# A two-direction selective scan on one core: the gate product issued after the scan of its slot, and the dt projection with its softplus moved by one slot

## The chip, the cores and the metric

The kernel runs on one core of one Trainium2 chip. The core has a matrix engine (PE, with a separate record for its weight loads, PEld), a vector engine (DVE), an activation engine (ACT), a general engine (POOL) and a queue that issues transfers (SP), each with its own instruction stream; sixteen DMA engines carry the transfers. The metric is the device time in microseconds (us). The time before is 8892.45 us, the median of three runs (8888.39 to 8895.94).

## The reference

The input is (1, 64, 256, 128): 64 channels, 256 times, 128 frequencies, in 32-bit floats. Layer 0 runs a pair of selective state-space blocks (one forward, one on the reversed sequence) along time, and then another pair along frequency. One block is, cut to what matters:

```python
xz = einsum('nld,ed->nle', rmsnorm(u), in_proj_w); x, z = split(xz, 2)
x  = silu(causal_conv4(x) + conv_b)
dt, B, C = split(x @ x_proj_w.T, [4, 4 + 16])
dt = softplus(dt @ dt_proj_w.T + dt_proj_b)
h_t = exp(dt_t * A) * h_{t-1} + dt_t * B_t * x_t      # 128 channels x 16 states
y_t = sum over states of h_t * C_t
out = ((y + x * Dp) * silu(z)) @ out_proj_w.T + u
```

The two directions are concatenated, projected to 64 channels and added to the input. Layer 1 is a normalisation, a convolutional LSTM over 32 windows and a projection. It isn't touched here.

## The kernel before

Layer 0 is done by the class `Stage`, once for time (stage 0, sequences of 256) and once for frequency (stage 1, sequences of 128). A stage has 64 **chunks** of 512 tokens. A chunk has 16 **slots**: two directions d of eight slots each, and each slot takes eight channels of all 16 states twice, as one tile of 128 partitions by 1024. The slot is named by its number in the chunk, 0 to 15.

The order of the work is written out by hand: `run` (L524) walks over all slots of a stage, and every engine takes its instructions in the order in which this loop writes them. In slot S it writes:

- `gate` (L480), when S is 2 or 10: y times silu(z), on DVE, for the direction that ended two slots before;
- `times_b` for S+1 on DVE (L437): the driving term, in PSUM, times B;
- `recur` on DVE (L443): the scan of 1024 steps, 2.28 us, that makes h;
- `outputs` for S-1 on POOL (L456): h times C;
- `inputs` for S+2 on PE (L416): it spreads dt*x over the states into one of three PSUM tiles `bx`, and `decays` for S+2 on ACT (L430): exp(A*dt), two activations into one of four tiles;
- `add_up` for S-2 on PE (L471), in odd slots: the sum over states of two h tiles into y. There is one y tile in PSUM, and its first matmul in a direction is L464;
- `close_a` in slot 2 (L491) and `close_b` and `keep` in slot 3 (L500, L510 or L517): the output projection of the chunk before, and its copy into X;
- at last the steps that prepare the next chunk, which `head` (L369) puts into slots.

The steps of `head` and the slot of the running chunk in which each stands:

| step | engine, line | slots before (d=0; d=1) |
|---|---|---|
| `squares`, `means`, `rms` | ACT L256, PE L261, ACT L266 | 12, 13 |
| `normalise` | POOL L272, then a copy of `unp` by DMA (L273), issued on SP | 14 |
| `project_x` | PE L281 and L282, reads `unp`; ACT L283 | 0; 4 |
| `project_z` | PE L288, ACT L296 | 1; 5 |
| `silus` | ACT, two table loads (L301, L306), four activations (L305) | 5 |
| `project_dt`, `softplus_a` | PE L310; ACT L321 to L323 (abs, relu, exp) | 6; 9 |
| `softplus_b` | ACT L329 to L331 (1+e, its log, and back) | 7; 10 |
| `softplus_c` | POOL L334, L335 | 8; 11 |
| `softplus_d` | POOL L339, then four writes of dt to DRAM (L343), issued on SP | 9; 12 |
| `times_x` | POOL L348 | 9; 12 |
| `project_bc` and `keep_bc`, first B, then C | PE L354, ACT L358 | 7, 8; 10, 11 |
| `spread_dt`, four of 1 MB in each direction | DMA L364 into three tiles `rep`, issued on SP | 10, 12, 14, 0; 2, 4, 6, 8 |

All projections of `head` and the output projection share one PSUM tile (tag `mm`), so each of them waits until the one before has been read. Where two steps stand in one slot, those of the earlier chunk come first, and within a chunk the order of the `put` calls holds. So in slot 14 the spread of dt stands on SP ahead of the copy of `unp`.

## Time and profile before

| what | value |
|---|---|
| median of three runs | 8892.45 us |
| profiled execution | 8909.66 us, its span 8907.9 us |
| busy PE, DVE, POOL, ACT | 7263.5, 7220.8, 6371.9, 5230.0 us |
| mean granted PE clock | 0.946 |
| span from 220 to 3950 us (most of stage 0): busy DVE, POOL, PE, ACT | 3385.4, 3024.2, 2976.9, 2475.3 of 3730 us |
| span from 8000 us (layer 1): busy PE | 894.2 of 908 us |

In the profile a row of a group gives the line, the engine, the operation and its tiles, the number of instructions, their busy time and mean duration in nanoseconds, and after the second bar the time the engine stood idle just before them with what ended most of it. In the timeline a row gives start, length, engine and line. SPq is the queue that issues transfers: its length is the time of issuing, and the data move later. The page's busy shares of the engines are means over the whole span. They don't say which of them sets the period of a chunk.

### The profile page before, as it was taken

The numbers are of one execution on the slowest core, as the hardware profiler recorded it, in microseconds if no ns is written. First come the engines' busy times: TensorE is split into PE (matmuls) and PEld (weight loads), VectorE is DVE, ScalarE is ACT, GpSimd is POOL, SyncE is SP. The second block draws the span as 40 slices with busy tenths as digits, with TensorE's granted clock in tenths as the row PEclk, the third lists the DMA queues.
The fourth block names the chain that finished last, engine by engine and source line by source line (L and its number), as shares of the span: only waits on it lengthen the run. The fifth ranks groups of instructions, "written<-read, shape, count | busy, mean of one in ns | idle before, by whom it ended". The sixth has DMA issues, their size and how long they took to land. (4 is left out here: it accounts for less than half of the span.)

```text
span 8907.9 us, 80273 instructions
## 1 busy us (share of the span) xinstructions
PE 7263.5 (82%) x24548; PEld 2187.8 (25%) x24548; DVE 7220.8 (81%) x4671; ACT 5230.0 (59%) x9321; POOL 6371.9 (72%) x3351
## 2 busy tenths in 40 slices
PE   7888787887888887868787878878787888599999
PEld 2222222222222222212222222222222222145554
DVE  6999999999999999969999999999999999711112
ACT  5666666666666666646666666666666666511111
POOL 5888888888888888868888888888888888511111
PEclk8999999999999999979999999999999999899999
DMA  5766676666666666656666666666666666400000
GB/s 126 160 153 151 157 161 156 154 155 158 157 156 150 159 159 153 154 115 154 152 149 152 156 151 151 154 155 150 149 157 151 151 153 154 106 13 9 9 9 10
DMA packets 238749, 1186.43 MB, mean 133 GB/s; under 512 B 39376, under 2 KB 64624, under 8 KB 107248
## 3 DMA queue, kind: packets, MB, share of 16 engines
q1 hardware_dynamic: 238320, 1181.30, 57.8%
q8 instruction: 197, 3.23, 0.2%
q14 instruction: 232, 1.90, 0.1%
HBM read 1088.88 MB, written 75.50 MB: 131 GB/s over the span
## 5 line engine op out<-in xcount | busy, mean ns | idle before, releaser
L456 POOL TENSOR_TENSOR h<-h,bc 128x1024 f32<-128x1024 f32 x2048 | 4807.9, 2360 | 942.9 <-DVE h L443 932.9
L443 DVE TENSOR_TENSOR_SCAN h<-dA,bx 128x1024 f32<-128x1024 f32 x2048 | 4659.7, 2275 | 0.0
L416 PE MATMUL bx<-dtx,sel 64*128 64x512 f32 x8192 | 2636.3, 680 | 504.6 <-DVE h L443 500.8
L430 ACT ACTIVATE dA<-rep,A 128x510 f32<-128x510 f32 (+1 forms) x4096 | 2699.8, 711 | 27.9 <-DVE h L443 24.6
L437 DVE TENSOR_TENSOR bx<-bx,bc 128x1024 f32<-128x1024 f32 x2048 | 2480.2, 1211 | 288.6 <-PE bx L416 235.9
L471 PE MATMUL y<-h,fold 128*32 128x512 f32 x8192 | 1364.2, 649 | 145.8 <-POOL h L456 145.8
L416 PEld LDWEIGHTS bx<-dtx,sel 64*128 64x128 f32 x8192 | 741.5, 195 | 2061.3 <-issue 1157.2
L354 PE MATMUL pb<-xs,wbc 128*128 128x512 f32 x1024 | 627.9, 697 | 440.1 <-ACT dt L322 253.8
L718 PE MATMUL pg<-xn,acc 128*128 128x456 f32 x2048 | 815.8, 549 | 0.7 <-ACT gxe L645 0.7
L755 POOL TENSOR_TENSOR a<-a,c 128x488 f32<-128x488 f32 x31 | 53.4, 1722 | 935.7 <-DVE n L777 794.9
L283 ACT ACTIVATE xs<-px,cb 128x512 f32<-128x512 f32 x256 | 176.0, 687 | 919.0 <-PE px L282 919.0
L777 DVE TENSOR_SCALAR n<-v,slope 128x512 f32<-128x512 f32 x64 | 31.1, 487 | 775.9 <-ACT v L775 774.8
L334 POOL TENSOR_TENSOR e<-e,w 128x512 f32<-128x512 f32 x256 | 326.9, 1277 | 454.2 <-ACT w L331 428.3
L482 DVE TENSOR_TENSOR yz<-y,zs 128x512 f32<-128x512 f32 x256 | 176.7, 690 | 446.4 <-PE y L471 446.1
L281 PE MATMUL px<-unp,g 128*128 128x512 f32 x512 | 305.0, 679 | 231.3 <-DMA unp<-unp 223.7
L310 PE MATMUL pv<-xs,wdt 128*128 128x512 f32 x512 | 303.5, 676 | 227.6 <-ACT xs L305 226.3
L471 PEld LDWEIGHTS y<-h,fold 128*32 128x32 f32 x8192 | 192.4, 111 | 1185.9 <-POOL h L456 585.3
L775 ACT ACTIVATE v<-pproj,bpr 128x512 f32<-128x512 f32 x32 | 22.0, 687 | 774.2 <-PE pproj L770 774.2
L718 PEld LDWEIGHTS pg<-xn,acc 128*128 128x128 f32 x2048 | 375.4, 188 | 372.3 <-issue 349.0
L354 PEld LDWEIGHTS pb<-xs,wbc 128*128 128x128 f32 x1024 | 159.8, 196 | 943.0 <-ACT dt L322 510.8
L358 ACT COPY bc<-pb 128x512 f32<-128x512 f32 x512 | 295.3, 577 | 112.9 <-PE pb L354 104.1
L348 POOL TENSOR_TENSOR dtx<-dt,xs 128x512 f32<-128x512 f32 x256 | 325.2, 1270 | 20.1
(129 smaller groups left out, 6164.1 us busy)
## 6 DMA issues: line engine op xcount, KB each, us to landing
rep<-there SPq DMA_DIRECT2D x1024, 1024.0 KB
there<-dt SPq DMA_DIRECT2D x1024, 64.0 KB
unp<-unp SPq DMA_DIRECT2D x128, 128.0 KB
u<-in_x SPq DMA_DIRECT2D x64, 128.0 KB
out<-y SPq DMA_DIRECT2D x32, 256.0 KB
w<-in_W_ih_f SPq DMA_DIRECT2D x5, 512.0 KB
w<-in_W_ih_b SPq DMA_DIRECT2D x5, 512.0 KB
cw<-in_conv_w SPq DMA_DIRECT2D x4, 128.0 KB
```

The lines of the kernel that those rows point to most:

```text
L281: nc.tensor.matmul(self.seqs(px), lhsT=m.G1[i], rhs=self.unp[:, :, first : first + L], start=True, stop=False)
L310: self.nc.tensor.matmul(self.pv, lhsT=self.m.Wdt[2 * self.stage + d], rhs=self.at["xs", ch, d], start=True, stop=True)
L334: self.nc.gpsimd.tensor_sub(self.e, self.e, self.w)
L348: self.nc.gpsimd.tensor_mul(dtx, self.dt, self.at["xs", ch, d])
L354: self.nc.tensor.matmul(self.pbc, lhsT=wt, rhs=self.at["xs", ch, d], start=True, stop=True)
L416: self.nc.tensor.matmul(bx[:, j], lhsT=self.m.sel[rows, r, k], rhs=dtx[rows], start=True, stop=True)
L430: nc.scalar.activation(dA[:, j, :, live], self.seqs(rep[:, r + 2 * j])[:, :, live], AF.Exp, scale=m.A[:, i, g : g + 1])
L437: self.nc.vector.tensor_mul(bx, bx, self.at["B", ch, d].unsqueeze(1).to_broadcast([P, 2, NTOK]))
L443: self.nc.vector.tensor_tensor_scan(h.rearrange("p j n -> p (j n)")[:, step], self.dA[S % NRING].rearrange("p j n l -> p (j n l)")[:, step ...
L456: self.nc.gpsimd.tensor_mul(h, h, self.at["C", ch, d].unsqueeze(1).to_broadcast([P, 2, NTOK]))
L471: nc.tensor.matmul(y[32 * r : 32 * r + 32], lhsT=m.fold[:, k], rhs=hs[r % 2][:, r // 2], start=False, stop=k == NK - 1, skip_group_check=True,
L718: nc.tensor.matmul(pg[:, :, 2 : 2 + inner], lhsT=acc[:, q, gate * P : (gate + 1) * P], rhs=xv[:, rows, half, q : q + inner], start=q == 0, ...
```

## The change

The `gate` of slots 2 and 10 is written after `recur` of the same slot instead of ahead of `times_b` and `recur`. In `head` the projection of dt with `softplus_a` moves from slots 6 and 9 to 7 and 10. For d=0 `softplus_b` stays in slot 7, straight after `softplus_a`, and `softplus_c` (8), `softplus_d` and `times_x` (9) stay; for d=1 all of these move one slot on, to 11, 12 and 13. The projections and copies of B and C move one slot on in both directions, to 8 and 9 and to 11 and 12. The spreads of dt stay in their slots.

```diff
         for d in range(2):
-            s = 6 + 3 * d
+            s = 7 + 3 * d
             put(s, self.project_dt, d)
             put(s, self.softplus_a, d)
-            put(s + 1, self.softplus_b, d)
+            put(s + d, self.softplus_b, d)
             put(s + 1, self.project_bc, d, 0)
             put(s + 1, self.keep_bc, d, 0)
-            put(s + 2, self.softplus_c, d)
+            put(s + 1 + d, self.softplus_c, d)
             put(s + 2, self.project_bc, d, 1)
             put(s + 2, self.keep_bc, d, 1)
-            put(s + 3, self.softplus_d, d)
-            put(s + 3, self.times_x, d)
+            put(s + 2 + d, self.softplus_d, d)
+            put(s + 2 + d, self.times_x, d)
             for k in range(4):
                 put(12 + 8 * d + 2 * k - 2, self.spread_dt, d, k)
...
-            if S % 8 == 2 and S > 8:
-                self.gate(*self.where(S - 8)[:2])
             if 0 <= S + 1 < last:
                 self.times_b(S + 1)
             if 0 <= S < last:
                 self.recur(S)
+            if S % 8 == 2 and S > 8:
+                self.gate(*self.where(S - 8)[:2])
```

## The prediction

> **What bounds the kernel now.** I read the groups of instructions first. They show DVE without a wait before its scan (L443) and with two waits before other work: 446.4 us before the gate product (L482), 288.6 us before the product with B (L437).

> ```profile
> L443 DVE TENSOR_TENSOR_SCAN h<-dA,bx 128x1024 f32<-128x1024 f32 x2048 | 4659.7, 2275 | 0.0
> L437 DVE TENSOR_TENSOR bx<-bx,bc 128x1024 f32<-128x1024 f32 x2048 | 2480.2, 1211 | 288.6 <-PE bx L416 235.9
> L334 POOL TENSOR_TENSOR e<-e,w 128x512 f32<-128x512 f32 x256 | 326.9, 1277 | 454.2 <-ACT w L331 428.3
> L482 DVE TENSOR_TENSOR yz<-y,zs 128x512 f32<-128x512 f32 x256 | 176.7, 690 | 446.4 <-PE y L471 446.1
> ```

> A chunk of 16 slots needs of DVE 16 x 3.31 us (scan to scan) plus 2 x 0.61 for the gates: 54.2 us. The gates of slot 2 follow each other in the timeline at 58.46 us in most chunks of stage 0 (58.70 in stage 1; the means with the disturbed chunks are 59.03 and 59.63). So each chunk has 4.3 us in which DVE isn't the bound, and the question is what closes that period. Here is the timeline of one chunk, cut to the steps that release one another (start, length, engine, line).

> ```profile
> 1996.94 1.28 POOL L334 TENSOR_TENSOR e<-e,w 128x512 f32<-128x512 f32 x1 [3.16 <-ACT w L331]
> 2013.96 1.28 POOL L339 TENSOR_TENSOR dt<-lw,dt 128x512 f32<-128x512 f32 x1
> 2015.27 1.72 SPq L343 DMA_DIRECT2D there<-dt  x4
> 2016.56 4.67 POOL L456 TENSOR_TENSOR h<-h,bc 128x1024 f32<-128x1024 f32 x2
> 2017.03 0.52 SPq L364 DMA_DIRECT2D rep<-there  x1
> 2021.20 1.27 POOL L272 TENSOR_TENSOR unp<-u,rs 64x512 f32<-64x512 f32 x1
> 2022.50 0.64 SPq L273 DMA_DIRECT2D unp<-unp  x1
> 2025.05 1.10 PE L281 MATMUL px<-unp,g 128*128 128x512 f32 x2 [1.65 <-DMA unp<-unp]
> 2029.16 0.69 DVE L482 TENSOR_TENSOR yz<-y,zs 128x512 f32<-128x512 f32 x1 [1.33 <-PE y L471]
> 2033.23 1.13 PE L416 MATMUL bx<-dtx,sel 64*128 64x512 f32 x4 [0.25 <-DVE h L443]
> 2042.44 1.12 PE L288 MATMUL pz<-unp,wz 64*128 64x512 f32 x2
> 2043.60 0.59 ACT L296 COPY zs<-pz 128x512 f32<-128x512 f32 x1 [1.14 <-PE pz L288]
> 2055.38 1.27 POOL L334 TENSOR_TENSOR e<-e,w 128x512 f32<-128x512 f32 x1 [3.15 <-ACT w L331]
> ```

> The reader is to see a closed loop in which each engine is back to back: POOL from its wait for softplus (1996.94) to the end of the normalise (2022.47), 25.5 us; the shift copy of unp to the first matmul on it, 2.6 us; PE from there (2025.05) to the end of the last z product (2043.56), 18.5 us with one gap of 0.26 us at 2033.23; ACT through silus, decays and both halves of softplus to POOL's next start, 11.8 us. Together 58.4, the period. The gate's wait at slot 2 (1.33) and the waits in slots 9 and 10 (0.82 and 1.84) are where DVE's slack shows. They are not what sets the period.

> Last, busy time in short stretches around the shift copy, issued at 2022.50. The three last fields are PE's granted clock, the DMA share and GB/s:

> ```profile
> 2018.00:2022.00 4.00, 2.82 (x12) 0.62 (x12) 4.00 (x3) 3.51 (x8) 4.00 (x3) 1.00 0.96 230
> 2022.50:2023.00 0.50, 0.50 (x4) 0.07 (x2) 0.50 (x1) 0.00 (x0) 0.50 (x1) 1.00 0.51 98
> 2023.00:2023.50 0.50, 0.40 (x2) 0.00 (x0) 0.50 (x1) 0.00 (x0) 0.50 (x1) 1.00 0.02 0
> 2024.00:2025.00 1.00, 0.00 (x0) 0.00 (x0) 1.00 (x2) 0.00 (x0) 1.00 (x2) 1.00 0.92 286
> 4095.00:4099.00 4.00, 4.00 (x8) 0.89 (x6) 1.96 (x1) 1.76 (x4) 4.00 (x3) 0.57 0.78 172
> ```

> The 1 MB spread (rep) issued at 2017.03 drains at about 2022.9; only then does the small copy move. It fits with no room to spare. The last line is another chunk, where PE had waited 1.93 us for unp: afterwards the granted clock is 0.57, and that chunk took 60.37.

> [...] laying its matmuls on a 3.41 us grid, all 74 windows busy under 0.40 are followed by a half-clock window, 117 of 165 between 0.40 and 0.50, and 32 of 1837 above 0.60.

> **The change part by part**, per chunk, with P the moment px can start (2025.05).

> *Gate behind the scan.* No instruction is added or removed. Product 3 now can start when inputs(3) ends (2028.07), not after add_up and gate (2029.77), 1.7 us sooner. But the next PE work isn't waiting for that: PE goes on with z product, inputs and close_a to about P+7.9, so inputs(5) starts at 2032.95 instead of 2033.23. Gain on the loop 0.3 us. The gate's own 0.61 comes after scan 2 (about P+6.4 to 7.1); what waits for it, the new y (P+8.9) and close_b (P+11), is later. With that cover gone it would cost up to 0.61. At slot 10 both the gate and its wait lie in slack: 0.

> *Softplus a and b together, one slot later (d=0).* ACT's work between silus and POOL's start is the same: two decays, six activations. Before, a decay stood between exp and the w that needs it (pitch 0.52); now they touch, and the dependent pitch of lw to w is 0.66 to 0.71: +0.17 us on the loop. The dt matmul, in slot 7 at about P+22.6 to 23.7, is ahead of ACT's need at about P+26.4 (z product's end 18.2, copy, table loads and silus 5.4, two decays 2.8): 0. The B and C products and copies one slot later are due at slots 15 and 17: 0. They leave PE and DVE small waits in slots 9 to 12, inside DVE's slack of over 4 us.

> *d=1 one slot later.* POOL's own sum stays 25.5, as the same products run in another order: outputs(12) now comes before softplus_d, not after times_x. So dt is ready one product (2.34) later, at 2017.6. With it on SP's queue, in order: four writes of dt (1.72) to 2019.3, then the 1 MB rep of slot 14, issued at 2019.4 instead of 2017.03, then unp, still issued at 2022.5. Rep takes 1.05 MB / 230 GB/s = 4.6 us from 1.2 us after its issue: 2020.6 to 2025.2. Unp's 0.13 MB, 1.1 us, ends at 2026.3 and px starts 0.45 later, at 2026.75: **+1.7 us** on the loop. Bounds: 0 if the small copy passes the large one, 4.6 if it waits for all of it.

> *What is late next: PE's clock.* PE's idle time before px grows from 1.65 to about 3.4 us. A grid of 3.41 us windows then has one with 0.55 or more idle in about 9 phases of 10. Stage 1 already shows the slope: with 1.93 us instead of 1.65, 26 of 62 chunks took over 60 us, against 9 of 61 in stage 0. One slow window on this back-to-back chain cost 60.37 - 58.70 = 1.65 us; some fall partly into the wait, so 0.92 x 1.4 = 1.3 a chunk. Of the present excess of the means (0.57 and 0.93, 0.75 together) I take all to be of this kind and subtract it: **+0.55**. Bounds: 0 and 1.65 + 1.65 (two windows).

> Sum: 1.7 - 0.3 + 0.17 + 0.55 = 2.1 us for each of 2 x 63 chunks that prepare a next one: 126 x 2.12 = 267 us. The profiled execution of 8909.66 (span 8907.9) becomes 9177. It stands 17 us above the median of 8892.45, which becomes 9160. The second layer, 900 us at the end, is untouched.

> **The rivals.**
> (B) The copy is late but the slow windows are no more than now: 126 x 1.57 = 198, 9090. For it: the grid's phase is free, and a longer loop could keep px off bad phases. Against: the idle time equals a whole window.
> (C) The copy isn't held up: 126 x (0.17 - 0.3) = -16, 8876, no change that counts. It needs unp to overtake rep, or rep to end by 2023.5; rep would have to move in 3 us what took 4.6.
> (D) The other side: the gate's wait is real loss and DVE is the bound. Then 446 us leave: 8446. It decides if product 3, ready 1.7 us sooner, moved PE's chain as much; at 2033.23 the profile shows only 0.26 us of it.
> (E) Both upper ends together, unp 4.6 late and two slow windows each time: 126 x (4.6 - 0.3 + 0.17 + 3.3 - 0.75) = 885, 9777. For it speaks only that both depend on the same wait.

> **Chances.** Forecast 0.58, B 0.25, C 0.08, D 0.05, E 0.04. Within the forecast the delay (1.3 to 2.1) and the slow windows (0 to 1.4 net) give 9080 to 9270; B reaches down to about 9030. The range 8990 to 9300 holds nearly all of these two, some 0.8. A difference of 0.2% (18 us) is about what this kernel's measurement can tell from none. Faster: D and a tail of C, 0.08; within 0.2%: the rest of C, 0.05; slower 0.87.

> **What would show it.** In the changed profile: the wait before L482 nearly gone, that before L437 grown beyond 446 + 289 us in place of it; L281's wait for unp, 223.7 us now, near 430; rep of slot 14 issued about 3 us before unp instead of 5.5; more half-clock windows just after px, mean clock under 0.946; scan and product durations unchanged. The prediction is wrong if px starts within 2.7 us of the normalise, if slot-2 gates stand closer than 58.4 us, or if PE has gaps between px and the last z product.

## The result and the profile after

The changed kernel takes 9306.45 us (median of four runs, 9298.78 to 9308.66) against 8894.19 us of the kernel before (8888.39 to 8897.46). The ratio is 1.0463, interval 1.0445 to 1.0481: it is 4.6% slower. The sign and the place were forecast, the size wasn't: 412 us were lost where 267 were predicted.

The profiled execution took 9298.78 us, with a span of 9297.0 and a mean granted PE clock of 0.918 (before: 8909.66, 8907.9 and 0.946). The span grew by 389 us, which is 3.1 us for each of the 126 chunks that prepare a next one. These are the groups of instructions after, as far as they changed or answer those shown of before, with the row of the first product on `unp` (L281):

```profile
L443 DVE TENSOR_TENSOR_SCAN h<-dA,bx 128x1024 f32<-128x1024 f32 x2048 | 4662.1, 2276 | 41.7 <-issue 41.7
L437 DVE TENSOR_TENSOR bx<-bx,bc 128x1024 f32<-128x1024 f32 x2048 | 2488.5, 1215 | 1047.1 <-PE bx L416 992.4
L281 PE MATMUL px<-unp,g 128*128 128x512 f32 x512 | 383.5, 840 | 477.0 <-DMA unp<-unp 377.2
L482 DVE TENSOR_TENSOR yz<-y,zs 128x512 f32<-128x512 f32 x256 | 170.4, 666 | 9.3 <-PE y L471 9.3
```

The work itself costs what it did: the scan takes 2.276 us, the product with B 1.215. DVE's wait of 446.4 us before the gate (L482) is 9.3 now. In its place the wait before the product with B grew from 288.6 to 1047.1, which is 312 us over the two waits of before together (735.0). A wait that moves like this says that DVE isn't the bound. Where the time goes shows in the row of L281. This is that row in the kernel before:

```profile
L281 PE MATMUL px<-unp,g 128*128 128x512 f32 x512 | 305.0, 679 | 231.3 <-DMA unp<-unp 223.7
```

PE's idle time before it was 231.3 us and is 477.0, and one such matmul now takes 840 ns instead of 679. PE comes later to this product, and then runs it at half clock more often: in both traces one such matmul takes 0.67 us in the median at a granted clock of 1.00 and 1.06 at 0.50, and 188 of the 512 ran wholly at 0.50 after, 30 before.

The timeline of one chunk after, cut to the steps of the loop (start, length, engine, line, and in brackets the idle time before it with its releaser):

```profile
2051.78 1.27 POOL L334 TENSOR_TENSOR e<-e,w 128x512 f32<-128x512 f32 x1 [4.19 <-ACT w L331]
...
2071.13 1.27 POOL L339 TENSOR_TENSOR dt<-lw,dt 128x512 f32<-128x512 f32 x1
2074.18 0.52 SPq L364 DMA_DIRECT2D rep<-there  x1
2076.02 1.26 POOL L272 TENSOR_TENSOR unp<-u,rs 64x512 f32<-64x512 f32 x1
2077.31 0.64 SPq L273 DMA_DIRECT2D unp<-unp  x1
2081.96 1.18 PE L281 MATMUL px<-unp,g 128*128 128x512 f32 x2 [2.15 <-POOL h L456]
2082.93 1.91 PE L282 MATMUL px<-unp,g 128*128 128x512 f32 x2
...
2086.67 1.23 DVE L437 TENSOR_TENSOR bx<-bx,bc 128x1024 f32<-128x1024 f32 x1 [3.39 <-PE bx L416]
2090.00 0.67 DVE L482 TENSOR_TENSOR yz<-y,zs 128x512 f32<-128x512 f32 x1
...
2101.83 0.59 ACT L296 COPY zs<-pz 128x512 f32<-128x512 f32 x1 [1.14 <-PE bx L416]
...
2113.74 1.27 POOL L334 TENSOR_TENSOR e<-e,w 128x512 f32<-128x512 f32 x1 [4.01 <-ACT w L331]
```

This is the loop of the prediction, and it can be read link by link. POOL, from its wait for softplus (2051.78) to the end of the normalise (2077.28), takes 25.5 us as before. The copy of `unp`, from there to the first matmul on it (2081.96), takes 4.7 us instead of 2.6. PE, from there to ACT's copy of the last z product (2101.83), takes 19.9 instead of 18.5. ACT, up to POOL's next start (2113.74), takes 11.9 instead of 11.8. On SP's queue the 1 MB spread was issued 3.1 us ahead of the copy of `unp`; before it was 5.5.

The busy time in short stretches around the copy shows the other half. A row gives the stretch and its length, the busy time of PE, PEld, DVE, ACT and POOL with the number of instructions, and at last PE's granted clock, the DMA share and GB/s:

```profile
2075.50:2079.50 4.00, 3.38 (x10) 0.70 (x10) 2.74 (x2) 0.00 (x0) 4.00 (x3) 0.51 1.06 254
2079.50:2081.90 2.40, 0.31 (x2) 0.00 (x0) 2.04 (x2) 0.00 (x0) 2.40 (x3) 1.00 1.02 205
2083.30:2084.30 1.00, 1.00 (x2) 0.00 (x0) 0.00 (x0) 0.00 (x0) 1.00 (x2) 0.50 0.94 213
```

In the first stretch the DMA engines are full with the spread (a share of 1.06; PE's granted clock is 0.51 there too). In the second, PE is busy for 0.31 of 2.40 us: it waits for `unp`. In the third, after this idle time, PE works at a granted clock of 0.50, in the middle of the chain that everything waits for.

I measured the four links in every chunk of the profiled executions. The table gives their means in us over the 63 chunks of a stage that prepare a next one (stage 0; stage 1), with those of four experiments that follow. The PE link ends at the start of ACT's copy of the last z product, so the four add up to the period by construction.

| kernel | POOL | copy of unp | PE chain | ACT to POOL's start | period |
|---|---|---|---|---|---|
| before | 25.40; 25.66 | 2.96; 2.86 | 18.83; 19.26 | 11.8 | 58.98; 59.56 |
| after | 25.39; 25.66 | 4.98; 4.69 | 20.22; 19.98 | 11.9 | 62.51; 62.25 |
| gate moved alone | 25.41; 25.67 | 2.87; 2.87 | 18.51; 18.51 | 11.8 | 58.57; 58.83 |
| after, spread behind unp | 25.39; 25.65 | 2.61; 2.62 | 18.66; 18.48 | 11.9 | 58.59; 58.68 |
| after, PE kept busy | 25.40; 25.67 | 5.26; 4.90 | 18.23; 18.11 | 11.9 | 60.81; 60.60 |
| normalise one slot sooner | 23.13; 23.39 | 4.73; 4.86 | 18.26; 18.23 | 11.8 | 57.90; 58.27 |

In the PE chain after, PE stands idle for only 0.04 us of 20.2 and 20.0 in the mean, and its granted clock there is 0.898 and 0.902 (before: 0.3 and 0.4 us idle, 0.985 and 0.961). So the longer chain is slower matmuls and not waits inside it.

### The profile page after: what moved, and what is told of

The parts are those of the page before. It is cut to its first block, busy times and chain, and to the rows that moved or that the text cites. A ratio compares the mean times of both kernels' runs of the same rounds, so it can differ in the third digit from the quotient of the medians.

```text
span 9297.0 us, 80527 instructions
## 1 busy us (share of the span) xinstructions
PE 7533.1 (81%) x24548; PEld 2253.7 (24%) x24548; DVE 7244.1 (78%) x4671; ACT 5267.7 (57%) x9321; POOL 6366.1 (68%) x3351
## 5 line engine op out<-in xcount | busy, mean ns | idle before, releaser
L456 POOL TENSOR_TENSOR h<-h,bc 128x1024 f32<-128x1024 f32 x2048 | 4799.6, 2357 | 1232.8 <-DVE h L443 1127.1
L443 DVE TENSOR_TENSOR_SCAN h<-dA,bx 128x1024 f32<-128x1024 f32 x2048 | 4662.1, 2276 | 41.7 <-issue 41.7
L437 DVE TENSOR_TENSOR bx<-bx,bc 128x1024 f32<-128x1024 f32 x2048 | 2488.5, 1215 | 1047.1 <-PE bx L416 992.4
L416 PE MATMUL bx<-dtx,sel 64*128 64x512 f32 x8192 | 2719.3, 684 | 445.5 <-DVE h L443 429.5
L430 ACT ACTIVATE dA<-rep,A 128x510 f32<-128x510 f32 (+1 forms) x4096 | 2698.6, 711 | 56.0 <-DMA rep<-there 35.1
L471 PE MATMUL y<-h,fold 128*32 128x512 f32 x8192 | 1512.0, 664 | 353.8 <-POOL h L456 352.7
L416 PEld LDWEIGHTS bx<-dtx,sel 64*128 64x128 f32 x8192 | 763.3, 195 | 2037.5 <-issue 1339.3
L281 PE MATMUL px<-unp,g 128*128 128x512 f32 x512 | 383.5, 840 | 477.0 <-DMA unp<-unp 377.2
L334 POOL TENSOR_TENSOR e<-e,w 128x512 f32<-128x512 f32 x256 | 327.9, 1281 | 557.9 <-ACT w L331 532.0
L471 PEld LDWEIGHTS y<-h,fold 128*32 128x32 f32 x8192 | 203.3, 112 | 1537.5 <-POOL h L456 782.7
L282 PE MATMUL px<-unp,g 128*128 128x512 f32 x512 | 366.4, 808 | 0.0
L296 ACT COPY zs<-pz 128x512 f32<-128x512 f32 x256 | 150.0, 586 | 347.6 <-PE bx L416 272.5
L335 POOL TENSOR_TENSOR lw<-lw,e 128x512 f32<-128x512 f32 x256 | 326.2, 1274 | 20.1
```

Of the source, the lines that this page charges most:

```text
L281: nc.tensor.matmul(self.seqs(px), lhsT=m.G1[i], rhs=self.unp[:, :, first : first + L], start=True, stop=False)
L282: nc.tensor.matmul(self.seqs(px), lhsT=m.G2[i], rhs=self.unp[:, :, second : second + L], start=False, stop=True)
L334: self.nc.gpsimd.tensor_sub(self.e, self.e, self.w)
L335: self.nc.gpsimd.tensor_add(self.lw, self.lw, self.e)
L416: self.nc.tensor.matmul(bx[:, j], lhsT=self.m.sel[rows, r, k], rhs=dtx[rows], start=True, stop=True)
L430: nc.scalar.activation(dA[:, j, :, live], self.seqs(rep[:, r + 2 * j])[:, :, live], AF.Exp, scale=m.A[:, i, g : g + 1])
```

## Experiments

### Which part of the change costs the time

Each experiment is set beside runs of the kernel before that were made next to it; their medians lie between 8886.84 and 8897.24 us.

Four kernels take the change apart. First the gate alone, on the kernel before:

```diff
-            if S % 8 == 2 and S > 8:
-                self.gate(*self.where(S - 8)[:2])
             if 0 <= S + 1 < last:
                 self.times_b(S + 1)
             if 0 <= S < last:
                 self.recur(S)
+            if S % 8 == 2 and S > 8:
+                self.gate(*self.where(S - 8)[:2])
```

> The kernel before with the gate alone moved behind the scan of its slot. Loop theory (the loss comes from the copy of unp queued behind the 1 MB spread, and from the halved PE clock after the longer wait): this part only takes 0.3 us off the loop, 126 x 0.3 = 38 us, so about 8856, and the copy still lands some 2.6 us after the normalise. Rival G (the gate behind the scan costs time): up to the whole 412 us, at least the 0.61 us of each of 256 gates, 9050 to 9306. Rival H (the steps of d=0 drawn together or moved make ACT and PE late in slots 7 to 10): no change, 8894.

It took 8838.28 us, 0.9937 of before (0.9922 to 0.9952). So this part is a gain of 56 us, where 38 were expected. The row of the product with B, in the groups of this kernel:

```profile
L437 DVE TENSOR_TENSOR bx<-bx,bc 128x1024 f32<-128x1024 f32 x2048 | 2488.1, 1215 | 606.8 <-PE bx L416 555.4
```

The wait before the gate is 8.9 us here, and the one in this row takes 318 us more than before: of the 437 us that the gate no longer waits, DVE waits 318 at the product with B. Another 30 went to new idle time before the scan and 12 to longer busy time. What is left, 77 us, is about the 74.5 by which this profiled execution's span (8833.4) is shorter.

Then the moves of `head` alone, with the gate left in its old place:

```diff
-            s = 6 + 3 * d
+            s = 7 + 3 * d
...
-            put(s + 1, self.softplus_b, d)
+            put(s + d, self.softplus_b, d)
...
-            put(s + 2, self.softplus_c, d)
+            put(s + 1 + d, self.softplus_c, d)
...
-            put(s + 3, self.softplus_d, d)
-            put(s + 3, self.times_x, d)
+            put(s + 2 + d, self.softplus_d, d)
+            put(s + 2 + d, self.times_x, d)
```

> The kernel before with the moved head steps alone, the gate where it was. Loop theory: the changed kernel without the 0.3 us a chunk that the gate gives, 9306 + 38 = about 9344; the copy lands 4.6 to 5 us after the normalise. Rival G: about 8894. Rival H: about 9306.

It took 9378.36 us, 1.0545 (1.0529 to 1.0561), 484 us more than before and 34 more than expected: the gate, worth 56 us alone, is worth some 72 beside these moves.

The smallest edit that holds the supposed cause moves only the end of softplus and dt\*x of d=1 from slot 12 to 13, in the kernel before:

```diff
-            put(s + 3, self.softplus_d, d)
-            put(s + 3, self.times_x, d)
+            put(s + 3 + d, self.softplus_d, d)
+            put(s + 3 + d, self.times_x, d)
```

> The kernel before with nothing changed but softplus_d and times_x of d=1 one slot later (12 to 13). Loop theory: this alone puts the writes of dt and the spread of slot 14 one POOL product later, so the whole loss is here: 2.0 us of copy and about 1.3 us of slow clock a chunk, about 9310. Rivals G and H: about 8894, since neither the gate nor the steps of d=0 are moved.

It took 9358.22 us, 1.0520 (1.0502 to 1.0537): 464 of the 484 us are in these two steps of one direction (48 us more than expected). Its timeline at the copy, cut to the two transfers and what stands around them:

```profile
2024.59 0.52 SPq L364 DMA_DIRECT2D rep<-there  x1
2026.42 1.27 POOL L272 TENSOR_TENSOR unp<-u,rs 64x512 f32<-64x512 f32 x1
2027.72 0.64 SPq L273 DMA_DIRECT2D unp<-unp  x1
2032.49 1.84 PE L281 MATMUL px<-unp,g 128*128 128x512 f32 x2 [3.85 <-DMA unp<-unp]
```

The spread is issued 3.13 us ahead of the copy, the first matmul on `unp` starts 4.80 us after the normalise ended, and the two of its line take 1.84 us instead of 1.10 (in the chunk of the changed kernel the two of L282 took 1.91 at a granted clock of 0.50).

The counter-test puts these two steps of d=1, and `softplus_c` with them, back into their old slots in the changed kernel, and leaves everything else as changed:

```diff
-            put(s + 1 + d, self.softplus_c, d)
+            put(s + 1, self.softplus_c, d)
...
-            put(s + 2 + d, self.softplus_d, d)
-            put(s + 2 + d, self.times_x, d)
+            put(s + 2, self.softplus_d, d)
+            put(s + 2, self.times_x, d)
```

> The changed kernel with softplus_c, softplus_d and times_x of d=1 back in slots 11 and 12; all else as changed (the gate, the dt projections, the two halves of softplus of d=0 together, the products with B and C). Loop theory: POOL's order and SP's order are those of before, so only the gate's gain and ACT's 0.14 us a chunk remain: the gate alone (8838) + 126 x 0.14 = about 8856. Rival H (the steps of d=0 and the later products of B and C take a share of the loss): 8900 or more.

It took 8850.68 us, 0.9956 (0.9939 to 0.9972). The dt projection one slot later, the softplus halves together and the later B and C products together cost 13 us over the gate alone (8838.28 beside 8894.24, and 8850.68 beside 8894.00), which the two intervals hardly tell from nothing.

### Is it the spread that stands ahead of the copy?

In the changed kernel, only the one spread that was put ahead of the copy of `unp` is issued a slot later, and so behind it. POOL's order stays, and nothing else moves.

```diff
-                put(12 + 8 * d + 2 * k - 2, self.spread_dt, d, k)
+                put(12 + 8 * d + 2 * k - 2 + (d == 0 and k == 2), self.spread_dt, d, k)
```

> The changed kernel with one of the eight spreads of dt (d=0, the third) issued in slot 15 instead of 14, so that on SP it stands behind the copy of unp instead of ahead of it. Loop theory: the copy lands about 2.3 to 2.6 us after the normalise again, PE's wait and the half-clock windows fall back to what they were, and only ACT's 0.14 us and the gate's gain of 0.3 remain: about 8875, at most 8930. Rivals G and H: nothing of what they blame is touched, so 9280 to 9310.

It took 8819.53 us, 0.9918 (0.9903 to 0.9932). The whole loss is gone: the kernel is 75 us faster than before, and 55 faster than was expected. The timeline at its copy, cut in the same way:

```profile
2012.74 1.27 POOL L272 TENSOR_TENSOR unp<-u,rs 64x512 f32<-64x512 f32 x1
2014.04 0.64 SPq L273 DMA_DIRECT2D unp<-unp  x1
2014.72 6.44 SPq L364 DMA_DIRECT2D rep<-there  x3
2016.63 1.10 PE L281 MATMUL px<-unp,g 128*128 128x512 f32 x2 [1.68 <-DMA unp<-unp]
```

The copy is first in the queue now, and PE starts 2.62 us after the normalise ended. The later spread still comes in time for the decays that read it: ACT's wait for the spreads before its decays (L430) is 32.0 us in all, and 35.1 in the changed kernel. This separates the order on SP from every other account: POOL's work, the later dt and the later B and C are all still there, and cost nothing that shows. It also takes away a loss that was there before: the copy now comes to PE 2.61 and 2.62 us after the normalise in the mean, against 2.96 and 2.86 before, and more than 2.8 us after it in 2 of 126 chunks against 35.

The spread behind the copy could have shared the DMA engines with it. To see whether it does, the spread of slot 0 was issued in slot 1 in the changed kernel:

```diff
-                put(12 + 8 * d + 2 * k - 2, self.spread_dt, d, k)
+                put(12 + 8 * d + 2 * k - 2 + (d == 0 and k == 3), self.spread_dt, d, k)
```

> The changed kernel with the spread that follows the copy of unp on SP (d=0, the fourth) issued one slot later, in slot 1 instead of 0. It asks why the copy came 2.0 us later and not the 1.7 of the prediction. If the copy shares the engines with the spread behind it: it lands some 0.3 us sooner, 126 x 0.3 = 38 us less than the changed kernel, about 9268. If only the spread ahead of it counts: no change, 9306.

It took 9308.05 us, 1.0465 (1.0446 to 1.0483), the time of the changed kernel, and its copy comes no sooner (5.07 and 4.79 us after the normalise). Of the spreads next to the copy, only the one ahead of it counts.

### How much of the loss is PE's clock?

Three extra matmuls stand ahead of the first product on `unp` of each chunk in the changed kernel. They write into the same PSUM tile, and the real product then overwrites what they wrote. The order on SP's queue stays, but they fill most of PE's idle time before it. The lines below them are numbered 4 higher.

```diff
+        for _ in range(3 if d == 0 else 0):
+            nc.tensor.matmul(
+                px, lhsT=m.Wdt[i], rhs=m.sel[:, 0].rearrange("p k q -> p (k q)"), start=True, stop=True
+            )
```

> The changed kernel with three more matmuls of 128x512 (each about 1.05 us, into the px tile, overwritten by the real product) ahead of the first x projection of each chunk, to keep PE active while it waits for the copy of unp. Clock theory: the copy still lands 4.6 to 5 us after the normalise, but the half-clock windows after it go; PE's chain from px to the last z product falls from 20.0 us to about 18.4, so 126 x 1.6 = 200 us less than the changed kernel, about 9105. Rival (the longer chain has another cause, say waits between PE and DVE, and the low clock falls on work with slack): 9290 to 9310, or more by up to 126 x 0.3 where the extra matmuls outlast the wait.

It took 9077.13 us, 1.0213 (1.0198 to 1.0228): 229 us less than the changed kernel (222 by the two ratios), with more work in it. Its timeline from the extra matmuls (L282) to the products on `unp` (L285, L286):

```profile
2081.72 2.84 PE L282 MATMUL px<-sel,wdt 128*128 128x512 f32 x6
2085.35 1.10 PE L285 MATMUL px<-unp,g 128*128 128x512 f32 x2 [0.78 <-DMA unp<-unp]
2086.29 1.02 PE L286 MATMUL px<-unp,g 128*128 128x512 f32 x2
```

The copy lands as late as ever: in the packet records of the trace its last packet ends 3.72 and 3.43 us after its issue in the median, against 3.73 and 3.47 in the changed kernel. The first product on it comes even later than there (5.26 and 4.90 us in the table), as in 64 of 126 chunks the extra matmuls outlast PE's wait. But the matmuls on it take 1.10 and 1.02 us for two, against 1.18 and 1.91 at a granted clock of 0.87 and 0.50 in the chunk of the changed kernel; the 1.10 is what two took at 1.00 in the kernel before. The PE chain falls by 1.99 us in stage 0 and 1.87 in stage 1, and the mean granted clock of the run is 0.945 instead of 0.918. That is what the clock costs in a chunk of the changed kernel. The late copy stays, and so do 1.83 and 1.04 us of the longer period, some of it the overhang of the extra matmuls; with the spread behind the copy both the delay and the slow chain went.

The same on the kernel before, with one such matmul, was to measure how much of before was lost to the clock already:

> The kernel before with one more matmul of 128x512 (about 1.05 us, overwritten by the real product) ahead of the first x projection of each chunk, inside PE's wait of 1.65 us. It measures how much of the excess of the mean chunk over the usual one (0.75 us in the prediction) is the halved clock after that wait: if all, 126 x 0.75 = 95 us, about 8800; if only what PE's chain shows above its usual length (0.28 us in stage 0, 0.73 in stage 1), about 64 us, 8830; the rest is then the copy's own landing, which this leaves. If the clock has no part in it, 8894 or a little more.

It took 8867.84 us (eight runs), 0.9967 (0.9957 to 0.9978): a gain of 26 us, less than was expected. The PE chain fell from 18.83 and 19.26 to 18.66 and 18.57, which is 54 us over all chunks, but `unp` came 0.19 us later in stage 0. So only some 0.2 to 0.7 us a chunk, and most of it in stage 1, could be had from the clock in the kernel before.

### Can the loop be shortened?

If the loop through POOL sets the period, fewer of POOL's products between softplus and the normalise must shorten it. On the kernel before, with the gate moved, the normalise goes from slot 14 to 13:

```diff
-        put(-2, self.normalise)
+        put(-3, self.normalise)
```

> The kernel before with the gate moved as in the change and the normalise with its copy of unp in slot 13 instead of 14, so ahead of outputs(13) on POOL and ahead of the third spread on SP. Loop theory: the copy lands before PE can use it; PE then gets to px after outputs(13), add_up(13) and inputs, some 0.4 us sooner than now and without a wait, so that fewer half-clock windows follow: 126 x (0.4 + about 0.4) = 100 us less than the gate alone (8838), about 8740. Rival (the chain through POOL's products isn't the bound): no change from 8838, or slower where ACT's rs comes late for the earlier normalise.

It took 8757.15 us, 0.9854 (0.9838 to 0.9870): 130 us faster than before, where the gate alone gave 56. Its row of the first product on `unp`:

```profile
L281 PE MATMUL px<-unp,g 128*128 128x512 f32 x512 | 299.6, 667 | 16.4 <-DMA unp<-unp 14.9 <-ACT zs L296 1.4
```

POOL's link fell by 2.28 us, one product, but the period by only 0.67 and 0.56. PE hardly waits for `unp` now (14.9 us in all), and yet it comes to it 4.73 and 4.86 us after the normalise. Its own earlier work stands ahead, the sum over states (L471) of slot 13, and this waits for POOL:

```profile
2046.37 1.06 PE L471 MATMUL y<-h,fold 128*32 128x512 f32 x6 [1.68 <-POOL h L456]
```

So the loop still goes through POOL, now by its h times C of slot 13 and PE's sum of it instead of the normalise and the copy.

Then POOL's four products of d=1 were taken out of the loop, with the normalise in slot 13 and the gate moved. First into slots 14 and 15, behind the normalise:

```diff
-            put(s + 2, self.softplus_c, d)
+            put(s + 2 + 3 * d, self.softplus_c, d)
...
-            put(s + 3, self.softplus_d, d)
-            put(s + 3, self.times_x, d)
+            put(s + 3 + 3 * d, self.softplus_d, d)
+            put(s + 3 + 3 * d, self.times_x, d)
```

> The kernel with the gate moved and the normalise in slot 13, and besides softplus_c of d=1 in slot 14 and softplus_d and times_x of d=1 in slot 15: POOL's four products for d=1 (5.1 us) and the writes of dt then stand behind the normalise and its copy, where the change had moved them towards it. Loop theory: the loop falls from 57.7 to about 52.6 us, below what DVE needs (54.2), so that DVE becomes the bound: 126 x (2.9 to 3.5) = 365 to 440 us less than with the normalise alone (8757), 8320 to 8390. Rival (another chain is close behind, PE's order or the deadlines of the d=1 terms): 8500 to 8750.

It took 9138.99 us, 1.0276 (1.0261 to 1.0292). This missed what was expected by over 700 us. Its timeline, cut to PE's sum over states (L471), the second half of the z product and ACT's copy of it:

```profile
2058.49 1.49 PE L471 MATMUL y<-h,fold 128*32 128x512 f32 x6 [2.63 <-POOL h L456]
2060.93 1.06 PE L288 MATMUL pz<-unp,wz 64*128 64x512 f32 x1
2062.02 0.59 ACT L296 COPY zs<-pz 128x512 f32<-128x512 f32 x1 [6.49 <-PE bx L416]
```

POOL's products of d=1 now stand in front of its h times C of slots 14 and 15. PE waits 2.63 us for that h in its sum over states, and the z product stands behind that sum on PE. So the work was moved out of one link and into another of the same loop, and the mean clock fell to 0.900. I had counted POOL's products between softplus and the normalise, and not who waits for those that came later.

Second, into slots 0 and 1 of the next chunk, in the same steps:

```diff
-            put(s + 2, self.softplus_c, d)
+            put(s + 2 + 5 * d, self.softplus_c, d)
...
-            put(s + 3, self.softplus_d, d)
-            put(s + 3, self.times_x, d)
+            put(s + 3 + 5 * d, self.softplus_d, d)
+            put(s + 3 + 5 * d, self.times_x, d)
```

> The kernel with the gate moved and the normalise in slot 13, and softplus_c of d=1 in slot 0 of the next chunk, softplus_d and times_x of d=1 in its slot 1: POOL's four products for d=1 (5.1 us) stand behind outputs(15), where the run before this one put them between outputs(13) and outputs(15), which PE's add_up(15) ahead of the z product waits for. Loop theory: those 5.1 us leave the way from softplus to PE's chain; the loop is then 52.8 to 54.8 us against DVE's 54.2, so that the period is 54.5 to 56: 8757 - 126 x (2.2 to 3.6) = 8300 to 8480. Rival (POOL's order isn't what closes the loop): 8750 or more, as with the run before this one (9139).

It took 8703.23 us, 0.9787 (0.9769 to 0.9804), the fastest kernel here, but 223 us above the upper end of what was expected. Its rows of the first product on `unp` and of the normalise:

```profile
L281 PE MATMUL px<-unp,g 128*128 128x512 f32 x512 | 297.7, 663 | 17.1 <-DMA unp<-unp 13.6 <-ACT dA L430 1.9 <-ACT zs L296 1.4
L272 POOL TENSOR_TENSOR unp<-u,rs 64x512 f32<-64x512 f32 x64 | 81.0, 1266 | 175.3 <-ACT rs L267 175.3
```

Here too PE hardly waits for `unp`. POOL waits for the root of the means (L267) ahead of the normalise instead, and DVE still waits 486.7 us before L437. What closes the period of this kernel isn't settled: from chunk to chunk it is 57.4 us in the mean, over DVE's 54.2, and its mean clock is 0.920, lower than before.

## Why the prediction was right and where it failed

**What bounds the kernel: right.** The loop POOL, copy, PE, ACT closes the period. This is shown by the experiments: one transfer issued behind the copy gave the whole loss back, and PE kept busy gave back its part. The links of the table, which add up by construction, say where the longer period lies: 2.02 (copy) - 0.01 (POOL) + 1.39 (PE) + 0.15 (ACT) = 3.55 in stage 0, and 1.83 + 0.00 + 0.72 + 0.15 = 2.70 in stage 1. The mean of these, 3.1, is what was 2.12 in the prediction.

| term, us per chunk | predicted | measured |
|---|---|---|
| copy of unp late | +1.7 | +2.02; +1.83 |
| gate moved, on PE's chain | -0.3 | -0.32; -0.46 (medians, gate alone) |
| softplus halves together | +0.17 | +0.15 |
| PE's clock, net | +0.55 | +1.71; +1.18 (PE chain, less the gate) |

**The gate: right.** It shortens PE's usual chain by 0.3 to 0.5 us, as forecast or a little more, and the wait goes where the prediction put it.

**The copy: mechanism right, size 0.1 to 0.3 short.** Rep was issued 3.0 to 3.3 us before `unp` instead of 5.4 to 5.7, as forecast. In the chunk shown, the working that gave 1.7 puts the first matmul at 2081.55, and it came at 2081.96. By the packet records the transfers took no longer than forecast: the copy's last packet ended at 2080.93, where the working has 2081.1. But from there to the first matmul it took 1.03 us, where the working has 0.45 (medians of all chunks: 1.03 and 1.09 after, 0.49 and 0.47 before). The spread behind the copy doesn't cause this, as issuing it later changed nothing. What does stays open. That the copy would wait for the spread ahead of it was an estimate of mine; the packet records show it for the changed kernel, where the copy's first packet moved 2.59 and 2.26 us after its issue in the median. In the kernel before it took 1.30 and 1.28, and one reading of it was off: in the chunk shown there the copy did not yet wait for the spread: its first packet moved at 2023.79, 1.3 us after its issue, with the DMA engines at a share of 0.02 from 2023.00 to 2023.50.

**The step that failed: PE's clock.** It went wrong twice, both times to the same side. First, 0.92 x 1.4 = 1.3 us gross was too small: with PE kept busy, the chain was 1.99 and 1.87 us shorter. I had taken 1.65 for one half-clock window from one chunk and cut it because "some fall partly into the wait". The clock record of the trace shows what happened instead: in each of the 126 chunks PE was at half clock inside this chain, for 4.06 us in the mean and in 41 of them for more than one window of 3.41 us. Half of that, 2.0 us, is about what the chain got longer. Second, I took the whole excess of the present means, 0.75, to be of this kind and subtracted it. The PE chain of before stands only 0.28 and 0.71 over its usual 18.55 (it has 1.09 us at half clock in the mean; half of that is 0.5). The rest was elsewhere: the copy's own landing was 2.96 and 2.86 in the mean and 2.63 and 2.62 in the median. Together these make +1.44 instead of +0.55, most of the missing 1.0 us. The claim behind it holds: the stretch from the product on `unp` of d=0 to that of d=1 is more than 1 us over its minimum in 34 of 126 chunks before, in 113 after, and in 3 with PE kept busy.

**The signs in the profile.** The wait before the gate vanished (9.3 us), and that before L437 grew beyond 735 (1047.1). The wait of L281 named for `unp` was 377.2 where near 430 was forecast; but its idle time in all, 477.0, grew by 246. In the chunk shown the wait is put down to POOL's L456 (98.4 us in all), but the product doesn't read what that line writes; it reads what the copy brings, and the copy's last packet ended only 1.03 us before it. PE has no gaps between px and the last z product (0.04 us in the mean). The mean clock fell to 0.918. Scan and products kept their durations.

**The rivals.** B, a late copy without more slow windows, has 1.57 us a chunk: the chunks lose twice that, and nearly half of it is the clock. C, a copy that isn't held up, falls with the 4.7 us in the timeline. D, the gate's wait as real loss, falls with the gate alone, which gains 56 and not 446 us. E, both upper ends, would be 7.0 us a chunk: the copy lost 1.9 of its 4.6, as it waits only for what is left of the spread, and the clock 1.9 of its 3.3.

## What to carry to other kernels

Find the loop that closes the period before pricing an edit, and price what the edit puts onto each of its links: a transfer issued one POOL product later cost 464 us over the chunks here, more than any instruction that was moved, because of what stands behind it on the same queue. A small transfer on such a loop belongs ahead of the large one that nobody waits for yet; here this order was worth 487 us (9306.45 against 8819.53). Idle time in front of a back-to-back PE chain cost a second time through the clock here (1.99 and 1.87 us a chunk), and that second term needs its own measurement, because in the kernel before it hides in a mean.
